# The last two row tiles of a gathered table: written from ScalarE's DMA queue instead of SyncE's, in a four-layer graph network

## The chip, the cores and the metric

The kernel runs on one core of one Trainium2 chip. Its time is the device time of one execution in microseconds. A core has five engines with queues of their own (PE is TensorE, DVE is VectorE, ACT is ScalarE, POOL is GpSimd, SP is SyncE) and 16 DMA engines that all queues share. Here SP and POOL issue DMAs; in the kernel before, ACT issues none.

## The reference

`x` is 2708 x 128, `adj` is 2708 x 2708, both float32. Four layers follow each other, each ending in `x = layernorm(x + layer(x, adj))`. The change lies in the first one:

```python
def _L0_gnn_ref(x, A, W1, b1, W2, b2, sigma, k):      # sigma 1, k 4
    z = _lap_mul(A, x) @ W1 + b1                        # _lap_mul: d * (A @ (d * x)), d = rowsum(A)**-0.5
    z = jax.nn.leaky_relu(z, negative_slope=0.1)
    ...                                                 # d2: squared distances of all rows of z
    S = jnp.exp(-jnp.sqrt(d2 + 1e-10) / (2.0 * sigma))
    S = jnp.where(ranks < k, S, 0.0)                    # the 4 nearest of each row
    A2 = S + A
    out = _lap_mul(A2, x) @ W2 + b2
```

Since `A2 = S + A`, the second product has two parts: the dense `A @ y2`, where `y2` is `x` scaled by the new row sums, and for each row a weighted sum of the rows of `y2` at its four nearest neighbours.

## The kernel before

**Tiling.** The 2708 rows are 22 row tiles (T = 22) of 128 rows, the last one of 20. The columns of the adjacency matrix are cut into six chunks c = 0 to 5 (C = 6) of 512, 512, 512, 512, 384 and 276. Of the transposed matrix the last six row tiles stay in SBUF (`res`); the other 16 (S = 16) are streamed in panels of four row tiles by one chunk, 1024 KB for a chunk of 512, into four slots of a buffer named `ring`. `load_panel` (L171) issues such a load on SP and takes the slots in turn. A slot can be loaded again when PE has read the panel in it.

**Neighbours.** A loop over the row tiles (L628) computes distances on PE, and DVE finds the nearest of each row (L649, L650). `weigh` (L590) turns them into weights and new row sums for a range of row tiles, scales `x` into `y2`, and writes these rows to `y2_rows` in HBM, the table from which neighbours are gathered (the profile calls it `y_rows`, since it leaves buffer numbers out). It is called three times: row tiles 0 to 16, 17 to 19, and last 20 and 21. The first two calls write from POOL's queue. The last call writes from SP's, in two DMAs: row tile 20 (L614, 64 KB) and the 20 rows of tile 21 (L618, 10 KB). Before that, ACT copies the 20 rows to two other partition groups (`spread`, L187).

**The pass over the panels.** `by_panels` (L189) goes through the chunks and, for each, through the row tiles: one product per row tile into the chunk's accumulator (L204), two PE instructions in the profile. For c = 0 four panels were loaded far ahead (`ready`), and the order of the row tiles is 0 to 11, 16 to 19, 12 to 15, 20: the last `y2` rows are needed last. From c = 1 on each panel is loaded into the slot that is freed by the panel four places ahead of it. The first of these loads (c = 1, panel 0, slot 0) is traced inside `with tc.issue_after(behind)`: on SP's queue it stands behind the last write to the table. This sets the order of issue only; it doesn't wait for the write to finish.

**The gather.** `sum_near` (L683) gathers three neighbour rows for each of the 128 rows of a tile with three indirect DMAs from POOL (L677), and DVE adds them up, weighted, into `near_sum` (L690). There are 22 x 3 = 66 gathers, with nine buffers (`got`). The first gather waits until all of the table has landed. When a chunk's products are done, `add_near` (L692) adds `near_sum` of its row tiles to the accumulator on PE (L697); then ACT copies the sum to `hT` (L837) and the linear layer follows (L725). For c = 0 these are row tiles 0 to 3, so gathers 1 to 12. PE, DVE and ACT keep the order that the source writes out here (`manual_schedule`, with the due times of the class `Due`); SP and POOL are ordered by the scheduler.

The order on SP around the change is, in the built program: panel 1 of c = 1 (slot 1), panel 2 (slot 2), the two writes, panel 0 (slot 0), panel 3 (slot 3).

Of the kernel before, what the change touches and what calls it, by code (L numbers as in the profile page):

```python
# [16 lines left out]
P = 128  # L17
# [35 lines left out]
def kernel(  # L53
# [16 lines left out]
    nc = tc.nc  # L70
    N, D = x.shape
    assert D == P
    T = (N + P - 1) // P
# [6 lines left out]
    FULL = N // P  # L80
    LAST = N - FULL * P
    S = T - RES
# [13 lines left out]
    def few(c):  # L96
        g = c % GROUPS * 32
        return slice(g, g + LAST)
# [12 lines left out]
    def acc_tile():  # L111
        return acc_pool.tile([P, CW], F32, tag="acc", name="acc")
# [58 lines left out]
    def load_panel(g, c, pool=None):  # L171

        if pool is None:
            s = slots[taken[0] % len(slots)]
            taken[0] += 1
        else:
            s = pool.tile([P, 4, CW], F32, tag="strip", name="part")
        nc.sync.dma_start(
            s[:, :, : cw[c]],
            adjT[g * 4 * P : (g + 1) * 4 * P, cols[c]].rearrange("(t p) k -> p t k", p=P),  # L180
        )
        return s
# [3 lines left out]
        for g in range(1, GROUPS):  # L186
            (engine or nc.scalar.copy)(rows[few(g)], rows[few(0)])  # L187

    def by_panels(weights, done, tick=None, ready=(), first=None, behind=None):  # L189

        ready = list(ready)
        accs = {}

        def product(c, i, src, w):
            lhsT = weights(i)[few(c) if i == FULL else slice(None)]
            start = c not in accs  # L200
            if start:
                accs[c] = acc_tile()
            stop = tick is None and i == (FULL if c % GROUPS == 0 else FULL - 1)
            nc.tensor.matmul(accs[c][: lhsT.shape[-1], :w], lhsT=lhsT, rhs=src, start=start, stop=stop)  # L204

        for c in range(C):
            w = cw[c]
            for i in [*(first if first and c == 0 else range(FULL)), *([FULL] if c % GROUPS == 0 else [])]:
                if i == FULL:
                    for n in range(c, c + GROUPS):  # L210
                        product(n, i, res[few(n), i - S, cols[n]], cw[n])
                    done(c, accs[c])
                    for _ in range(GROUPS if tick is not None else 0):
                        tick()
                    continue
                if i < S:
                    if i % 4 == 0:
                        if ready:
                            part = ready.pop(0)
                        elif behind is not None:  # L220
                            with tc.issue_after(behind):
                                part = load_panel(i // 4, c)
                            behind = None
                        else:
                            part = load_panel(i // 4, c)
                    src = part[:, i % 4, :w]
                else:
                    src = res[:, i - S, cols[c]]
                product(c, i, src, w)
                if i == FULL - 1 and c % GROUPS:  # L230
                    done(c, accs[c])
                if tick is not None:
                    tick()
# [8 lines left out]
    def rows_of(y):  # L242
        return lambda i: y[:, i, :]
# [122 lines left out]
    y2_rows = dram.tile([N, D], F32, tag="y2_rows", name="y2_rows")  # L366
    xw_rows = dram.tile([N, D], F32, tag="xw_rows", name="xw_rows")
    with tc.tile_pool(name="knn", bufs=1) as knn:
# [68 lines left out]
        due = Due()  # L437
# [28 lines left out]
        with (  # L466
# [5 lines left out]
            for c in range(C):  # L472
# [31 lines left out]
                t0, t1 = ts[0], ts[-1] + 1  # L504
# [53 lines left out]
        y2 = big.tile([P, T, D], F32, tag="y", name="y2")  # L558
# [31 lines left out]
        def weigh(ts):  # L590

            t0, t1 = ts[0], ts[-1] + 1
            nr, sm = near[:, t0:t1, :TOPK], sim[:, t0:t1, :]

            nc.vector.tensor_add(nr, nr, nsq[:, t0:t1, None].to_broadcast([P, t1 - t0, TOPK]))
            nc.vector.tensor_scalar(nr, nr, 0.0, DIST_EPS, op0=ALU.min, op1=ALU.subtract)
            nc.scalar.activation(sm, nr, AF.Ln, scale=-1.0)
            nc.scalar.activation(sm, sm, AF.Exp, scale=0.5)
            nc.scalar.activation(sm, sm, AF.Exp, scale=-0.5)
            dd = d2inv[:, t0:t1]  # L600
            nc.vector.tensor_reduce(dd, sm, AX.X, ALU.add)
            nc.vector.tensor_add(dd, dd, deg[:, t0:t1])  # L602
            nc.scalar.activation(dd, dd, AF.Ln)
            nc.scalar.activation(dd, dd, AF.Exp, scale=-0.5)
            if t1 < T:
                nc.gpsimd.tensor_mul(
                    y2[:, t0:t1, :], xs[:, t0:t1, :], d2inv[:, t0:t1, None].to_broadcast([P, t1 - t0, D])
                )
            else:
                scale_rows(y2, xs, d2inv, ts)  # L610
                spread(y2[:, FULL, :])
            full = min(t1, FULL)
            queue = nc.gpsimd if t1 < T else nc.sync
            ins = queue.dma_start(  # L614
                y2_rows[t0 * P : full * P, :].rearrange("(t p) d -> p t d", p=P), y2[:, t0:full, :]
            )
            if full < t1:
                ins = queue.dma_start(y2_rows[FULL * P :, :], y2[:LAST, FULL, :])  # L618
            else:
                for a in range(t0, t1, 11):  # L620
                    others(range(a, min(a + 11, t1)), nc.gpsimd)
            return ins.ins

        ready = [load_panel(g, 0) for g in range(G)]
        tc.keep_in_program_order(nc.scalar.preload_act_table_set("natural_log_exp_and_others"))
        with tc.tile_pool(name="keys", bufs=3) as keys:

            for n, t in enumerate([*range(4, S), *range(4), *range(S, T)]):  # L628
                p = pw[t]
                z2 = small.tile([P, P], F32, tag="z", name="z2")  # L630
                nc.scalar.mul(z2[:, :p], zT[:, t * P : t * P + p], 2.0)

                key = keys.tile([P, N], F32, tag="key", name="key")
                pks = [acc_tile() for _ in range(C)]
                def norms(c):
                    cs = cols[c]
                    nc.tensor.matmul(pks[c][:p, : cw[c]], lhsT=ones3[:, :p], rhs=nsq3[:, cs], start=True, stop=False)  # L637


                if n:  # L640
                    for c in range(C):
                        norms(c)
                for c in range(C) if n else (5, 3, 2, 4, 1, 0):
                    if not n:
                        norms(c)
                    cs = cols[c]
                    nc.tensor.matmul(pks[c][:p, : cw[c]], lhsT=z2[:, :p], rhs=zT[:, cs], start=False, stop=True)  # L647
                    nc.scalar.copy(key[:p, cs], pks[c][:p, : cw[c]])  # L648
                nc.vector.max(near[:p, t, :], key[:p])  # L649
                nc.vector.max_index(where[:p, t, :], near[:p, t, :], key[:p])  # L650
                if t == T - 6:
                    weigh(range(0, T - 5))
                if t == T - 3:
                    weigh(range(T - 5, T - 2))
            written = weigh(range(T - 2, T))
            others(range(T - 2, T), nc.vector)

    psum.close()
# [162 lines left out]
    due = Due()  # L821
# [50 lines left out]

    with tc.manual_schedule(engines={nc.tensor.engine, nc.vector.engine, nc.scalar.engine}):
        by_panels(
            rows_of(y2), end_pass2, due.tick, ready, [*range(S - 4), *range(S, T - 2), *range(S - 4, S), T - 2], written
        )
        due.flush()
    late.close()
# [6 lines left out]
    ready = [load_panel(g, c) for c, g in panels[: len(slots)]]  # L885
# [15 lines left out]
    with tc.tile_pool(name="rank", bufs=1) as rank:  # L901
# [254 lines left out]
        def weights(lw, n0):  # L1156

            g_all = turned(g_col, n0)
            n1 = min(n0 + 4, NQ)
            m = 2 * (n1 - n0)  # L1160
            b0 = 2 * n0
            w = lw[:, b0 : b0 + m, 2:]
            g = g_all[:, : m * (BJ + 2)].rearrange("p (b j) -> p b j", b=m)[:, :, 2:]
            if n0 // 4 in (1, 3):
                for n in range(m):
                    b = b0 + n
                    nc.scalar.activation(
                        w[:, n], g[:, n], AF.Relu, scale=slot_e[:, b : b + 1], bias=slot_f[:, b : b + 1]
                    )
                return  # L1170
            nc.vector.tensor_mul(w, g, slot_e[:, b0 : b0 + m, None].to_broadcast([P, m, BJ]))
            nc.vector.tensor_add(w, w, slot_f[:, b0 : b0 + m, None].to_broadcast([P, m, BJ]))
            nc.vector.tensor_scalar_max(w, w, 0.0)
# [55 lines left out]
        for c in range(C):  # L1229
            w = cw[c]  # L1230
            begins = c % GROUPS == 0
            for i0 in range(0, FULL - 1, 4):
                if i0 < S:
                    n = c * G + i0 // 4
                    part = ready[n] if n < len(ready) else load_panel(i0 // 4, c)
# [388 lines left out]
```

## Time and profile before

| | us |
|---|---|
| median of three runs | 1066.62 (1063.95 to 1068.74) |
| the profiled execution | 1068.2 |
| its span, first to last instruction | 1066.5 |
| PE busy | 990.4 (93% of the span) |
| DVE, ACT, POOL busy | 643.2, 339.1, 265.6 |
| DMA, mean over the span | 178 GB/s |

The profiled execution is 1.6 above the median and 1.7 longer than its span. All times of instructions below are of this execution, counted from the start of its span. A busy share is a mean over stages with different limits; what the change is worth has to be read from the stage around it, some 50 us from 290 on, in which the pass over the panels begins. In the part of the page that cuts the span in 40 slices, each slice is 26.7 us long; slices 12 and 13 are this stage. Bytes moved there go from 22 GB/s (slice 11) to 199 and 211.

### The profile page before, as it was taken

The page shows a single profiled execution, that of the slowest core. Times are in us where ns is not written, and L with a number is a line of the kernel's source. Part 1 is how long each engine was busy: PE and PEld are TensorE (multiplying, and loading weights), DVE is VectorE, ACT ScalarE, POOL GpSimd, SP SyncE. Part 2 cuts the span into 40 slices and gives each one's busy share as a digit, 9 for nine tenths or more (in the row PEclk, how much of TensorE's full clock was granted, in tenths as well). Part 3 has the DMA queues.
Part 4 walks back from the last instruction along what each step waited for, and adds up shares of the span by engine and source line. Part 5 has one row for each costly group of instructions (what it writes and reads, how often), then busy time and mean ns, then how long its engine had stood idle before and what let it go on. Part 6 is the DMA issues. An engine that isn't in the chain of part 4 may idle for free.

```text
span 1066.5 us, 11423 instructions
## 1 busy us (share of the span) xinstructions
PE 990.4 (93%) x3678; PEld 479.8 (45%) x3678; DVE 643.2 (60%) x1351; ACT 339.1 (32%) x614; POOL 265.6 (25%) x332
## 2 busy tenths in 40 slices
PE   0898999999998999699899999999999999999996
PEld 0345554444434566444333333334444544564444
DVE  5985438999954678764789999995121111132222
ACT  0000125555510235603767777663010100010000
POOL 4000000000447664107774444440121100000000
PEclk9989999999999999699999999999999999999998
DMA  9999350000056756399655546456765856575652
GB/s 338 367 342 249 115 166 1 0 1 1 22 199 211 239 175 207 126 341 306 165 160 131 147 135 164 137 151 208 226 198 173 291 196 202 159 256 170 225 173 67
DMA packets 109363, 190.30 MB, mean 178 GB/s; under 512 B 13650, under 2 KB 46690, under 8 KB 109294
## 3 DMA queue, kind: packets, MB, share of 16 engines
q1 hardware_dynamic: 91582, 151.86, 43.8%
q0 software_dynamic: 17712, 37.62, 12.7%
q8 instruction: 31, 0.51, 0.2%
q14 instruction: 38, 0.31, 0.1%
HBM read 214.37 MB, written 4.16 MB: 205 GB/s over the span
## 4 chain that ended last, share of the span: by engine, by line
PE 80%; DMA 7%; DVE 6%; issue 2%; POOL 2%; ACT 2%; SPq 1%; POOLq 0%; DVEq 0%; ACTq 0%
PE acc L204 34%; PE acc L647 9%; PE hacc L1285 9%; PE num L1428 9%; PE acc L432 7%; DMA res<-in_adjT 3%; PE acc L637 3%; PE acc L1181 2%; DMA got<-y_rows,where 1%; PE mis L289 1%; DMA part<-in_adjT 1%; DVE mask L784 1%; DVE both L487 1%; POOL ring L125 1%; PE mis L1192 1%
## 5 line engine op out<-in xcount | busy, mean ns | idle before, releaser
L1306 POOL DMA_INDIRECT ring<-in_adjT,slot_i x88 | 98.1, 1115 | 101.0 <-PE num L1428 84.8
L1428 PE MATMUL num<-ring,lw 128*64 128x512 f32 (+1 forms) x528 | 113.6, 551 | 3.6 <-DVE err L1270 1.8
L1285 PE MATMUL hacc<-inv,xws 128*128 128x512 f32 (+1 forms) x264 | 111.7, 559 | 0.5 <-ACT inv L1263 0.3
L647 PE MATMUL acc<-zT,z 128*128 128x512 f32 (+4 forms) x264 | 108.5, 558 | 0.0
L1260 ACT ACTIVATE inv<-num,plain 128x1024 f32<-128x1024 f32 x88 | 80.6, 916 | 59.3 <-PE num L1428 58.1
L257 POOL TENSOR_TENSOR rstd<-rstd,minus_half 128x4 f32<-128x4 f32 (+1 forms) x19 | 18.2, 957 | 313.3 <-DVE rstd L256 313.3
L648 ACT COPY key<-acc 128x512 f32<-128x512 f32 (+3 forms) x132 | 70.2, 535 | 59.7 <-issue 29.8
L238 ACT COPY gb<-acc 128x512 f32<-128x512 f32 (+2 forms) x18 | 9.6, 535 | 249.4 <-PE acc L204 249.4
L204 PE MATMUL acc<-ring,y 128*128 128x512 f32 (+2 forms) x192 | 81.8, 555 | 1.6 <-DMA ring<-in_adjT 1.1
L1270 DVE TENSOR_TENSOR err<-inv,num 128x1024 f32<-128x1024 f32 x88 | 74.4, 853 | 13.3 <-ACT inv L1263 12.5
L1285 PEld LDWEIGHTS hacc<-inv,xws 128*128 128x128 f32 x264 | 46.5, 189 | 77.5 <-issue 37.6
L677 POOL DMA_INDIRECT got<-y_rows,where x66 | 70.1, 1063 | 32.8 <-DMA y_rows<-y 9.3
L1277 DVE SCALAR_TENSOR_TENSOR inv<-gb,g_inv,inv 128x1024 f32<-128x1024 f32 x88 | 77.0, 913 | 0.1
L204 PE MATMUL acc<-ring,xs 128*128 128x512 f32 (+2 forms) x192 | 76.7, 542 | 0.0
L204 PE MATMUL acc<-ring,carry 128*128 128x512 f32 (+2 forms) x192 | 74.5, 542 | 0.0
L204 PE MATMUL acc<-ring,m_rows 128*128 128x512 f32 (+2 forms) x192 | 74.3, 542 | 0.0
L1274 DVE SCALAR_TENSOR_TENSOR inv<-err,inv 128x1024 f32<-128x1024 f32 x88 | 72.6, 863 | 0.1
L647 PEld LDWEIGHTS acc<-zT,z 128*128 128x128 f32 (+1 forms) x264 | 47.6, 188 | 54.9 <-issue 49.5
L1263 ACT ACTIVATE inv<-inv 128x1024 f32<-128x1024 f32 x88 | 67.6, 768 | 2.8
L649 DVE MAX8 near<-key 128x8 f32<-128x2708 f32 (+1 forms) x22 | 65.5, 2978 | 4.8 <-ACT key L648 4.8
L574 POOL TENSOR_TENSOR slot_e<-near,sim 128x44 f32<-128x44 f32 (+2 forms) x3 | 0.7, 244 | 271.5 <-DVE d2inv L602 267.3
L650 DVE FIND_INDEX8 where<-near,key 128x8 uint32<-128x2708 f32 (+1 forms) x22 | 65.4, 2972 | 0.0
(327 smaller groups left out, 1340.0 us busy)
## 6 DMA issues: line engine op xcount, KB each, us to landing
ring<-in_adjT SPq DMA_DIRECT2D x86, 1024.0 KB
ring<-in_adjT SPq DMA_DIRECT2D x19, 768.0 KB
part<-in_adjT SPq DMA_DIRECT2D x12, 1024.0 KB
ring<-in_adjT SPq DMA_DIRECT2D x19, 552.0 KB
res<-in_adjT SPq DMA_DIRECT2D x4, 1280.0 KB
more<-in_adjT SPq DMA_DIRECT2D x4, 1024.0 KB
part<-in_adjT SPq DMA_DIRECT2D x3, 768.0 KB
part<-in_adjT SPq DMA_DIRECT2D x3, 552.0 KB
```

What stands on the lines that cost most here:

```text
L204: nc.tensor.matmul(accs[c][: lhsT.shape[-1], :w], lhsT=lhsT, rhs=src, start=start, stop=stop)
L432: nc.tensor.matmul(accs[c][:, : cw[c]], lhsT=y[:, i, :], rhs=src[:, : cw[c]], start=first, stop=last)
L647: nc.tensor.matmul(pks[c][:p, : cw[c]], lhsT=z2[:, :p], rhs=zT[:, cs], start=False, stop=True)
L648: nc.scalar.copy(key[:p, cs], pks[c][:p, : cw[c]])
L677: nc.gpsimd.indirect_dma_start(out=got[:p, :], out_offset=None, in_=y2_rows[:, :], in_offset=bass.IndirectOffsetOnAxis(ap=where[:p, t, k : ...
L1260: nc.scalar.activation(inv, num[:, :w], AF.Ln, scale=plain[:, 0:1], bias=plain[:, 1:2])
L1270: nc.vector.tensor_mul(err, inv, num[:, :w])
L1274: nc.vector.scalar_tensor_tensor(inv, err, 2.0, inv, op0=ALU.subtract, op1=ALU.mult)
L1277: nc.vector.scalar_tensor_tensor(inv, gb[:, col : col + w], g_inv[:, q : q + 1], inv, op0=ALU.max, op1=ALU.mult)
L1285: nc.tensor.matmul(haccs[:, o:e], lhsT=xws[:, q, :], rhs=inv[:, o:e], start=(q == 0), stop=(q == NQ - 1))
L1306: nc.gpsimd.indirect_dma_start(out=rows[i][:KC, n, :], out_offset=None, in_=adj_half[:, :], in_offset=bass.IndirectOffsetOnAxis(ap=slot_i[ ...
L1428: nc.tensor.matmul(num[n * (BJ + 2) : (n + 1) * (BJ + 2), o:e], lhsT=lw[:, 2 * q + n, :], rhs=rows[i][:, n, c0 + o : c0 + e], start=True, ...
```

## The change

The last call of `weigh` writes from ACT's queue instead of SP's. `weigh` no longer hands back its last DMA, `by_panels` loses the parameter `behind`, and the first load of c = 1 is an ordinary `load_panel`.

```diff
-    def by_panels(weights, done, tick=None, ready=(), first=None, behind=None):
+    def by_panels(weights, done, tick=None, ready=(), first=None):
...
                         if ready:
                             part = ready.pop(0)
-                        elif behind is not None:
-                            with tc.issue_after(behind):
-                                part = load_panel(i // 4, c)
-                            behind = None
                         else:
                             part = load_panel(i // 4, c)
...
-            queue = nc.gpsimd if t1 < T else nc.sync
-            ins = queue.dma_start(
+            queue = nc.gpsimd if t1 < T else nc.scalar
+            queue.dma_start(
                 y2_rows[t0 * P : full * P, :].rearrange("(t p) d -> p t d", p=P), y2[:, t0:full, :]
             )
             if full < t1:
-                ins = queue.dma_start(y2_rows[FULL * P :, :], y2[:LAST, FULL, :])
+                queue.dma_start(y2_rows[FULL * P :, :], y2[:LAST, FULL, :])
...
-            return ins.ins
...
-            written = weigh(range(T - 2, T))
+            weigh(range(T - 2, T))
...
-            rows_of(y2), end_pass2, due.tick, ready, [*range(S - 4), *range(S, T - 2), *range(S - 4, S), T - 2], written
+            rows_of(y2), end_pass2, due.tick, ready, [*range(S - 4), *range(S, T - 2), *range(S - 4, S), T - 2]
```

In the built program SP now issues the panels of c = 1 in the order 0, 1, 2, 3. ACT issues the two writes right behind the two copies of `spread` and ahead of the copy L837. The order of all other instructions on PE, DVE, ACT and POOL is the same.

## The prediction

> **What bounds the kernel now.** The page's first part says PE:
>
> ```profile
> span 1066.5 us, 11423 instructions
> PE 990.4 (93%) x3678; PEld 479.8 (45%) x3678; DVE 643.2 (60%) x1351; ACT 339.1 (32%) x614; POOL 265.6 (25%) x332
> ```
>
> So the change can pay only where PE stands still. The waits of 280 to 345 us, the stage around the change, show where (waiting engine and line, what it waited for; us, times, longest):
>
> ```profile
> ACT hT L837 <- PE acc L697: 29.3, 1, 29.3
> ...
> POOL got L677 <- DMA y_rows<-y: 9.3, 1, 9.3
> ...
> PE acc L697 <- DVE near_sum L690: 4.0, 1, 4.0
> ...
> PE acc L204 <- DMA ring<-in_adjT: 1.1, 1, 1.1
> ```
>
> PE waits twice: 1.1 us for a panel and 4.0 us for the gathered sums of c = 0. Third view: the chain of waits in this stretch, which names the origin of the longer one (start, us, what):
>
> ```profile
> 294.84 10.55 PE acc L204 x24
> ...
> 305.41 0.37 SPq L178
> ...
> 305.83 0.50 SPq L614
> ...
> 306.38 6.41 DMA y_rows<-y
> ...
> 313.68 0.31 POOL got L677
> ...
> 319.04 5.45 DMA got<-y_rows,where
> ...
> 326.85 6.18 DMA got<-y_rows,where
> ...
> 333.92 0.49 PE acc L697 x2
> ```
>
> Read it downwards. The write of tile 20 stands on SP behind the load of slot 2, which waits until PE has read that slot (305.4). Both writes land at 306.38 + 6.41 = 312.8. POOL then starts the gathers (313.68), one each 1.30 us; the eleventh takes 6.2 us to land, and PE goes on at 333.92. So **the write, and not PE, sets the time here**. The panel wait is in PE's timeline:
>
> ```profile
> 312.08 2.09 PE L204 MATMUL acc<-res,y 128*128 128x512 f32 x8
> 315.30 14.00 PE L204 MATMUL acc<-ring,y 128*128 128x512 f32 x32 [1.13 <-DMA ring<-in_adjT]
> 329.14 0.83 PE L697 MATMUL acc<-ident,near_sum 128*128 128x128 f32 x6
> 333.92 0.49 PE L697 MATMUL acc<-ident,near_sum 128*128 128x128 f32 x2 [3.95 <-DVE near_sum L690]
> ```
>
> Last, stretches of 1 us behind the second wait (span, length, busy of the engines, then PE's granted clock, DMA share, GB/s):
>
> ```profile
> 335.00:336.00 1.00, 1.00 (x3) 0.49 (x2) 0.10 (x1) 0.98 (x2) 0.70 (x2) 0.68 0.36 123
> 336.00:337.00 1.00, 1.00 (x4) 0.48 (x4) 0.64 (x2) 0.34 (x1) 0.96 (x1) 0.50 0.29 82
> 337.00:338.00 1.00, 1.00 (x6) 1.00 (x6) 0.40 (x1) 0.00 (x0) 0.74 (x1) 0.50 0.23 57
> 338.00:339.00 1.00, 1.00 (x5) 0.64 (x4) 0.49 (x2) 0.00 (x0) 0.69 (x2) 0.61 0.08 25
> ```
>
> The wait has an after-effect: 0.32 + 0.50 + 0.50 + 0.39 = **1.7 us** of PE time lost to a halved clock. In this trace gaps of 1.13, 1.82 (at 515) and 1.87 us (735) leave the clock at 1.00; gaps of 2.16 (417), 2.30 (461) and 3.95 halve it. From about 2 us of idling on, it costs 1.7 more.
>
> [...] No run of before shows ACT's ring. [...] the panel in front of the write had moved its bytes by about 310 (383 + 240 + 389 + 379 GB/s in the four microseconds from 306), the write landed 2.7 us later.
>
> **The change, part by part.**
>
> *Panel 0 of c = 1 goes first.* PE frees slot 0 after four of the first twelve row tiles: 294.84 + 4 x 10.55/12 = 298.4. SP is idle then and issues at once, instead of at 306.78. The DMA moves 0 GB/s from 300 to 303, so nothing is in its way. A panel of 1.05 MB at the 400 GB/s of 310 to 312 takes 2.6 us[...]: it lands near 305 and is needed at 314.17. **PE's wait of 1.13 us goes**, and PE reaches L697's last two matmuls (row tile 3) at 329.97 - 1.13 = 328.84. Panels 1 and 2 keep their times (slots 1 and 2 free at 302.0 and 305.4), panel 3 (312.1) too. By itself this brings nothing: PE would wait 5.1 us for the sums instead of 3.95.
>
> *The two writes on ACT.* ACT ends the copies L187 at 305.1 and issues there (0.50 and 0.36 us, SP's durations): start 305.15 and 305.7 instead of 305.83 and 306.38. The waits that the built program gives them are on loads for c = 0, long landed: the page shows 0 to 1 GB/s from 160 to 267. Behind them on ACT stands only the copy L837, which PE releases at 334.4; with 29.3 us of idling there, 0.9 us of issue costs nothing. SP loses the same 0.9, free too.
>
> *When do the writes land?* Not shown in the trace, so bounded. Lower: like a gather of 64 KB with nothing beside it (2.6 us from issue, the fourth: 317.73 to 320.3), 305.7 + 2.9 = 308.6. POOL's own write of 192 KB (issued 303.47; the similar L768 write of 256 KB takes 4.1) is in by about 308, so it doesn't gate. Upper: the slot 2 panel (issued 305.41) goes first on each engine, and the write lands 2.5 us after its last byte at 310.1: 312.6, as before. Between: gathers that become ready while a panel flows take 5.0 to 6.2 us, giving 310.7 to 311.9. I take **310.5**, a little below these since the first write is issued before slot 2's load. The first gather then starts 0.87 later, as now: 311.4 instead of 313.7, **2.3 us earlier**.
>
> *What the gathers make of it.* The twelfth is issued at 328.16 - 2.3 = 325.9. In the way are the panels of c = 2, issued when PE frees slots, now from 317.6, 321.1, 324.5 and 328.0, that is 1.13 earlier than before. Relative to them the gathers gain 1.2 us. If all gathers keep their delays, the sums are ready 2.3 us earlier, 331.6; if they slip before the fourth panel, up to 1 more. I take 2.6: PE goes on at **331.3**. Its gap is then 331.3 - 328.84 = 2.5 us, above 2, so the half clock stays. Up to here no gain is counted twice: the 1.13 lies inside the 2.6.
>
> *Behind it.* From 334 to 415 PE is busy throughout (20.0 of 20 us in each stretch from 340 to 400), and DVE, ACT, the slots of the ring and the later gathers (from the 37th on they wait for free buffers) hang on PE or on the same first gather, so they move along. No late thing in the way: the sums of c = 1 are used at 355.1, their last gather was issued at 343.8. I keep 2.6, and 0.3 more for the chance that the gap falls below 2 us: **3 us**.
>
> Sum: 1066.5 - 3 = 1063.5 for the span, 1065.2 for the profiled execution of 1068.2. That one stood 1.6 above the median, so for a median I subtract the 3 from 1066.6: **1063.6**. The runs of before spread by 4.8 us; what a measurement can tell from no change is about 0.5%, 5.3 us.
>
> **The rivals.**
>
> *Early write.* Both writes pass between the panels of slots 1 and 2 and land at 309.5 or before. Gathers start 3.3 us earlier or more, the twelfth is out before 325 and the sums are there by 330.7. PE's gap falls below 2 us, the clock stays full: 3.2 + 1.7 = 4.9, at most 5.1 + 1.7 = 6.8. Time 1060 to 1061.7. For it: slot 2's load follows the first write only by a little on the engines. Against it: the second write is issued after that load.
>
> *Hidden anyway.* The write gets its turn only behind slot 2's panel and lands near 312.6. Then the gathers gain 0.2, at most 1.1 with the panels: 1065.5 to 1066.4. [...] This is also how the change would fail to do what it says.
>
> *Starved write, slower.* On ACT's own ring the write is no longer ahead of any panel. If the engines pass it over until the panel of slot 3 (issued 312.1, bytes 314.0 to 316.8) is through, it lands at 316.8 + 2.5 = 319.3 and everything behind it is 6.5 late; in exchange the gathers then meet fewer panels and the last ones take 2.7 instead of 5.3 to 6.2, so PE goes on near 337.5: 3.6 slower, 1070. One more panel, 3.4 us apart, and it is 7 slower, 1073.6. The point is a landing at 312.8. Against it: the DMA is idle of panels from about 310 to 314 now.
>
> **How the numbers follow.** Forecast as above (gain 1.5 to 4.5): 0.45. Early write: 0.25. Hidden: 0.15. Starved: 0.15. Faster by over 5.3 us: half of the early cases and their spread in measurement, with the upper edge of the forecast, 0.27. Slower by over 5.3: the starved cases of two panels, and one panel with an unlucky spread, 0.15. Within: 0.58. The range takes the early case to its end and the starved one to its first step: 1059 to 1070.5.
>
> **What would show it.** Right: no wait L204 <- DMA ring near 314; the chain still goes through the write, now from ACT, landing at 309 to 312; first gather near 311.4; PE on L697 after a gap of 2 to 3 us; half clock behind it. Wrong: a landing after 312.8; a gap of 4 us or more on L697; or the gain up to 340 lost again by 440.

## The result, and the profile after

Nine runs of the changed kernel have a median of 1061.78 us (1059.55 to 1066.67); nine of the kernel before, on the same chip, have 1068.75 (1063.95 to 1073.10). The ratio is 0.9937, with a 95% interval of 0.9918 to 0.9957: **6.7 us faster, at least 4.6 and at most 8.8**. The forecast was 3.

The first part of the page, and one row of its DMA queues (packets, MB, share):

```profile
span 1064.9 us, 11424 instructions
PE 993.3 (93%) x3678; PEld 481.3 (45%) x3678; DVE 642.9 (60%) x1351; ACT 338.8 (32%) x614; POOL 266.7 (25%) x332
...
q10 hardware_dynamic: 174, 0.08, 0.0%
```

The queue q10 is new: the 74 KB of the two writes, on ACT's own queue. The span is only 1.6 shorter, since the profiled execution (1066.67) is the slowest of its nine; the end of this section shows where it loses time. First the waits of the stage, 280 to 345 us (us, times, longest):

```profile
ACT hT L832 <- PE acc L692: 23.9, 1, 23.9
DVE near_sum L685 <- DMA got<-y_rows,where: 17.1, 10, 4.2
...
POOL got L672 <- DMA y_rows<-y: 4.5, 1, 4.5
```

POOL waits 4.5 us for the table instead of 9.3. No row of PE waiting for the sums or for a panel is left. The chain of waits from 294 to 340 says the same: of write and gathers nothing stands in it.

```profile
293.35 33.26 PE acc L204 x80
326.60 0.89 PE acc L692 x8
327.50 1.72 PE acc L204 x4
329.21 0.89 PE mis L720 x8
```

Next ACT's, POOL's, DVE's and PE's timelines, from which the times of the steps are read (start, us, engine, line; in brackets the idle time before it):

```profile
302.98 0.30 ACT L187 COPY y<-y 20x128 f32<-20x128 f32 x1 [0.49 <-DVE y L260]
302.99 0.34 ACTq L610 DMA_DIRECT2D y_rows<-y  x1
303.30 0.30 ACT L187 COPY y<-y 20x128 f32<-20x128 f32 x1
303.38 0.61 ACTq L614 DMA_DIRECT2D y_rows<-y  x1
327.53 0.58 ACT L832 COPY hT<-acc 128x512 f32<-128x512 f32 x1 [23.94 <-PE acc L692]
...
307.39 1.14 POOL L672 DMA_INDIRECT got<-y_rows,where  x1 [4.55 <-DMA y_rows<-y]
...
326.20 0.74 DVE L685 SCALAR_TENSOR_TENSOR near_sum<-got,sim,near_sum 128x128 f32<-128x128 f32 x2 [0.20 <-DMA got<-y_rows,where]
...
312.60 14.00 PE L204 MATMUL acc<-ring,y 128*128 128x512 f32 x32
326.44 1.05 PE L692 MATMUL acc<-ident,near_sum 128*128 128x128 f32 x8
327.33 1.88 PE L204 MATMUL acc<-res,y 128*128 128x512 f32 x4
```

The pass over the panels begins at 293.35 here and at 294.84 before; another kernel that is the same up to there begins at 293.19, so the change isn't the cause. From here on a time with a plus is counted **from the start of the pass**, PE's first product on L204, so that executions can be compared. ACT issues at +9.64 and +10.03, with the first copy and not behind the copies. The first gather starts at +14.04 instead of +18.84. The last two sums of row tile 3 end at 326.20 + 0.74 = 326.94, or +33.59, where PE went on at +39.08 before. PE reaches these two matmuls near 327.1, after six of the eight, with no gap: **the sums come 0.2 us before they are needed**. PE's transposes L737 start at +42.60, those of before (L742) at +49.69, **7.1 us earlier**. That is 1.13 of panel wait, 3.95 of waiting for sums, 1.7 of half clock, and 0.3 of small pieces, for this pair of executions; how far others differ is told with the experiments.

One-microsecond stretches of the same execution (PE's granted clock is the third value from the end):

```profile
327.00:328.00 1.00, 1.00 (x7) 0.72 (x6) 0.14 (x1) 0.47 (x1) 0.82 (x1) 1.00 1.11 406
328.00:329.00 1.00, 1.00 (x3) 0.38 (x2) 0.02 (x1) 0.98 (x2) 0.70 (x2) 1.00 0.98 260
...
460.00:461.00 1.00, 1.00 (x9) 1.00 (x8) 1.00 (x2) 0.00 (x0) 0.00 (x0) 0.75 1.05 389
461.00:462.00 1.00, 1.00 (x7) 1.00 (x6) 1.00 (x2) 0.00 (x0) 0.00 (x0) 0.50 1.04 387
...
967.00:968.00 1.00, 1.00 (x3) 0.40 (x3) 0.00 (x0) 0.00 (x0) 0.00 (x0) 0.50 0.00 0
```

Behind the sums the clock stays at 1.00. But this execution has half clock from 460 to 468 and again from 965 to 973, with PE busy all the time. The trace of before has neither; what it has at 461 comes directly behind a gap of 2.30 us, and its counterpart here, behind a gap of 2.16, is from 453 to 457. Added up over all stretches of a microsecond from 290 on (one minus the clock, times PE's busy time), the half clock costs 16.0 us here and 10.5 before; these two take 3.4 each. Without them, by this estimate, the execution would have taken 1066.67 - 6.8 = 1059.9, close to the fastest of the nine. So the lead of the stage isn't given to another wait: in this one execution it is taken back by a clock that falls elsewhere, with no gap of PE directly ahead of it. At 417 of before, the first gap of PE behind the pass, the lead is whole: the same matmul stands at +122.44 before and at +115.36 after, still 7.1.

### The profile page after: what moved, and what is told of

The parts are those of the page before. It is cut to its first block, busy times and chain, and to the rows that moved or that the text cites. A ratio compares the mean times of both kernels' runs of the same rounds, so it can differ in the third digit from the quotient of the medians.

```text
span 1064.9 us, 11424 instructions
## 1 busy us (share of the span) xinstructions
PE 993.3 (93%) x3678; PEld 481.3 (45%) x3678; DVE 642.9 (60%) x1351; ACT 338.8 (32%) x614; POOL 266.7 (25%) x332
## 4 chain that ended last, share of the span: by engine, by line
PE 81%; DVE 5%; DMA 5%; POOL 3%; issue 3%; ACT 2%; SPq 1%; POOLq 0%; DVEq 0%; ACTq 0%
PE acc L204 36%; PE acc L642 9%; PE hacc L1280 9%; PE num L1423 8%; PE acc L428 7%; DMA res<-in_adjT 3%; PE acc L1176 2%; PE acc L632 2%; PE mis L285 1%; DMA part<-in_adjT 1%; DVE mask L779 1%; DMA ring<-in_adjT,slot_i 1%; DVE both L483 1%; POOL ring L125 1%; PE mis L1187 1%
## 5 line engine op out<-in xcount | busy, mean ns | idle before, releaser
L204 PE MATMUL acc<-ring,y 128*128 128x512 f32 (+2 forms) x192 | 82.0, 557 | 0.5 <-POOL sim L579 0.5
L204 PE MATMUL acc<-ring,xs 128*128 128x512 f32 (+2 forms) x192 | 78.2, 551 | 0.0
L204 PE MATMUL acc<-ring,carry 128*128 128x512 f32 (+2 forms) x192 | 74.5, 542 | 0.0
L204 PE MATMUL acc<-ring,m_rows 128*128 128x512 f32 (+2 forms) x192 | 74.3, 542 | 0.0
```

## The experiments

The theory after the result: what counts is that the write is on its way **before the load of slot 2**, which is issued when PE has freed that slot (+10.57 in before). ACT's queue brings it there. Rivals: ACT's own queue as such; the early load of panel 0, which no longer stands behind the writes on SP. All kernels were timed beside the kernel before (median 1068.81 of 37 runs for the first four, 1068.61 of 59 for the others).

| | first write, second write | first gather | PE's gap on the sums | transposes | ratio, 95% | us |
|---|---|---|---|---|---|---|
| before | SP +10.99, +11.54 | +18.84 | 3.95 | +49.69 | | |
| after | ACT +9.64, +10.03 | +14.04 | none | +42.60 | 0.9937 (0.9918 to 0.9957) | -6.7 |
| e1_sp_no_order | SP +10.99, +11.54 | +18.03 | 2.85 | +47.72 | 0.9993 (0.9979 to 1.0006) | -0.7 |
| e2_act_panel0_late | ACT +9.64, +10.03 | +14.15 | none | +44.14 | 0.9943 (0.9922 to 0.9964) | -6.1 |
| e3_sp_write_first | SP +9.63, +10.03 | +12.45 | none | +42.60 | 0.9956 (0.9930 to 0.9983) | -4.7 |
| e4_pool | POOL +9.91, +10.49 | +16.46 | 2.65 | +47.22 | 0.9965 (0.9951 to 0.9980) | -3.7 |
| e5_act_late | ACT +9.64 (10 KB), +12.55 (64 KB) | +17.50 | 3.83 | +48.38 | 0.9999 (0.9985 to 1.0012) | -0.1 |
| e6_filled_gap | SP +10.99, +11.53 | +17.95 | 0.66 behind the filling | +47.26 | 0.9991 (0.9975 to 1.0007) | -1.0 |
| e7_add_later | SP +10.99, +11.53 | +16.86 | none | +47.76 | 0.9950 (0.9924 to 0.9977) | -5.3 |
| e8_after_add_later | ACT +9.64, +10.03 | +14.07 | none | +47.76 | 0.9964 (0.9949 to 0.9979) | -3.8 |

The last column is (ratio - 1) times the median of before. For e1 to e6 it and the column of the transposes agree within the interval; that of e3 is the loosest (7.1 in the trace, 1.8 to 7.5 in time). In e7 and e8 the transposes have six more row tiles ahead of them, so their column can't be compared.

One trace of before is a thin base. In e6 and e7, SP issues the panels and the writes around this place at the same times as in before (within 0.01 us), and yet the table lands earlier (POOL's timelines of e6 and e7):

```profile
312.58 1.14 POOL L677 DMA_INDIRECT got<-y_rows,where  x1 [8.45 <-DMA y_rows<-y]
...
311.71 1.14 POOL L677 DMA_INDIRECT got<-y_rows,where  x1 [7.35 <-DMA y_rows<-y]
```

The first gather starts at +17.95 and +16.86 there, against +18.84 in before, and PE's panel wait is 0.23 us in e6 and missing in e7. With the write from ACT (after, e2, e8) it is +14.04 to +14.15. So before is the slowest of three executions in this stage: the change brings the first gather forward by 2.7 to 4.8 us, and 7.1 us is what this pair of traces gives, not a constant.

**e1_sp_no_order**: panel 0 freed from the writes, but the writes on SP as before (diff against the changed kernel).

```diff
-            queue = nc.gpsimd if t1 < T else nc.scalar
+            queue = nc.gpsimd if t1 < T else nc.sync
```

> The writes stay on SP, but the load of panel 0 of c = 1 no longer stands behind them (SP's order: panels 0, 1, 2, the two writes, panel 3). Theory 'place of the write': PE's wait of 1.1 us for the panel goes, the write still stands behind panel 2's load and lands about 8 to 9 us after DVE has the rows of y2 (before 8.8, after 4.0), PE's gap at L692 grows to about 5 us, the half clock stays: 0 to 1 us faster than before. Rival 'order of the panels': the freed panel load is what pays, so at least 1.1 us and up to half of the 6.7 us measured, 2 to 4 us faster.

SP's timeline and PE's wait of this kernel:

```profile
300.33 3.80 SPq L178 DMA_DIRECT2D ring<-in_adjT  x2
304.18 0.50 SPq L610 DMA_DIRECT2D y_rows<-y  x1
304.73 0.36 SPq L614 DMA_DIRECT2D y_rows<-y  x1
...
330.27 0.49 PE L692 MATMUL acc<-ident,near_sum 128*128 128x128 f32 x2 [2.85 <-DVE near_sum L685]
```

The panel wait is gone, and PE still waits for the sums, which come 2 us earlier (+37.08 against +39.08). The gap did not grow to 5 us, as expected, but shrank to 2.85. How much of this is the freed panel and how much the spread between executions, one trace can't say: the first gather, at +18.03, lies within the +16.86 to +18.84 of before, e6 and e7. In the time nothing shows. This half of the change, alone, brings at most 2.2 us.

**e2_act_panel0_late**: the writes on ACT as in the change, but panel 0 of c = 1 is issued behind panels 1 and 2 (diff against the changed kernel, cut; `loads` collects the DMAs of `load_panel`).

```diff
+                        elif first and c == 1 and i == 0:
+                            n = taken[0]
+                            taken[0] = n + 1
+                            ready = [load_panel(g, c) for g in (1, 2)]
+                            taken[0] = n
+                            with tc.issue_after(loads[-1]):
+                                part = load_panel(0, c)
+                            taken[0] = n + 3
```

> The writes go from ACT as in the changed kernel, but panel 0 of c = 1 is queued on SP behind panels 1 and 2, as before the change. Theory 'place of the write': the write lands about 4 us after DVE has the rows, no gap above 1 us at L692 and no half clock there; a wait of 0 to 1 us for the panel comes back near 314: 5.5 to 7 us faster than before. Rival 'order of the panels': without it the gain is at most half, 3 us or less.

```profile
314.31 14.00 PE L206 MATMUL acc<-ring,y 128*128 128x512 f32 x32 [1.28 <-DMA ring<-in_adjT]
328.14 1.24 PE L702 MATMUL acc<-ident,near_sum 128*128 128x128 f32 x8
```

PE's timeline again: the panel wait is back, with 1.28 us, and behind it no gap for the sums. So the other half, the early write, carries nearly all of the gain: 6.1 us in time, 5.6 in the trace.

**e3_sp_write_first**: the kernel before, with the writes on SP, but with the first three panels of c = 1 behind them.

```diff
-                        elif behind is not None:
+                        elif behind is not None and c == 1 and i < 12:
                             with tc.issue_after(behind):
                                 part = load_panel(i // 4, c)
-                            behind = None
```

> The writes stay on SP but stand ahead of the loads of panels 0, 1 and 2 of c = 1 (in the kernel before only panel 0 is behind them). Theory 'place of the write': nothing is ahead of the writes, they land about 4 us after DVE has the rows; panel 0 is issued at about 306 and lands by 312, before its need at 314; 6 to 7 us faster than before, like the changed kernel. Rival 'ring of its own': only another ring than the panels' gets the write through; in SP's ring, with 3 MB of panels right behind it, it lands later than 6 us after the rows, and the gain is 3 us or less.

SP's and POOL's timelines:

```profile
303.83 0.35 SPq L613 DMA_DIRECT2D y_rows<-y  x1
304.23 0.38 SPq L617 DMA_DIRECT2D y_rows<-y  x1
304.71 1.49 SPq L178 DMA_DIRECT2D ring<-in_adjT  x3
...
306.65 1.44 POOL L676 DMA_INDIRECT got<-y_rows,where  x1 [2.95 <-DMA y_rows<-y]
```

SP's queue does it too: same times of issue as on ACT, gathers even 1.6 us earlier. The difference between the two is that here the loads of panels 0 and 1 stand behind the write as well: the first of them is issued at 304.71, and from 304 to 306 the DMA moves 303 KB, little more than the three writes to the table (272 KB), so hardly any of a panel passes with the write. PE's transposes start at +42.60, as in the change: with no gap left, earlier sums are worth nothing. So **ACT's queue isn't needed: a write issued as early, ahead of the panels, does it on SP**.

**e4_pool**: the last call of `weigh` writes from POOL's queue, like the first two (`queue = nc.gpsimd`).

> The last two row tiles are written from POOL's queue, like the rest of the table, with SP's panel order of the changed kernel. Theory 'place of the write': POOL is idle there, the writes have no panel ahead of them; two issues of about 0.9 us each instead of ACT's 0.3 and 0.6, so they land about 5 us after the rows of y2 are there, 1 us later than from ACT; gap at L692 about 1 us, no half clock: 5 to 6.5 us faster than before. Rival 'ring of its own': POOL's ring also carries its 192 KB write of row tiles 17 to 19, issued 1 us earlier, so the writes land at 7 us or more; half the gain, 3 us.

```profile
303.22 0.58 POOL L610 DMA_DIRECT2D y_rows<-y  x1 [0.40 <-DVE slot_e L578]
303.80 0.57 POOL L614 DMA_DIRECT2D y_rows<-y  x1
309.77 1.13 POOL L672 DMA_INDIRECT got<-y_rows,where  x1 [5.40 <-DMA y_rows<-y]
...
329.90 0.78 PE L692 MATMUL acc<-ident,near_sum 128*128 128x128 f32 x2 [2.65 <-DVE near_sum L685]
330.47 3.32 PE L204 MATMUL acc<-res,y 128*128 128x512 f32 x4
```

POOL's and PE's timelines. It issues only 0.3 and 0.5 us later than ACT, but the rows land 2.4 us later (first gather +16.46), and PE gets a gap of 2.65 with a half clock behind it: four matmuls of L204 take 3.32 us instead of 1.88. Whether the delay comes from POOL's own 192 KB write before them or from slot 2's load, issued in the same microsecond, no run tells apart. The expectation (a gap of about 1 us, no half clock) missed, and issuing ahead of slot 2's load is not always enough: both writes are issued before it (+10.57), and still land late. This is the outcome that the prediction gave to the change, gap, half clock and gain (3.7 us).

**e5_act_late**: the change, but seven idle copies on ACT (L609, in place) hold the 64 KB write back until 2.0 us after the issue of slot 2's load (+10.57).

```diff
                 spread(y2[:, FULL, :])
+                for _ in range(7):
+                    nc.scalar.copy(y2[:, t0, :], y2[:, t0, :])
```

> The changed kernel, with seven copies of row tile 20 of y2 onto itself on ACT ahead of its write (L610's), each waiting for the one before: the 64 KB write is issued some 2 to 3 us later, at about 12 us after the start of the pass, behind the issue of panel 2's load (10.6) instead of ahead of it (9.6). [...] it lands 3 to 4.5 us after issue, first gather at 16 to 17.5 us after the start of the pass (before 18.8, after 14.0), gap at L692 about 2 to 3 us with the half clock: 2 to 4 us faster than before. Rival 'a panel that flows is drained first, ACT's ring or not': it lands behind panel 2 as SP's write does, first gather at 18 us or more, gap about 4 us: 0 to 2 us faster than before.

```profile
302.42 2.28 ACT L609 COPY y<-y 128x128 f32<-128x128 f32 x7
304.72 0.36 ACTq L612 DMA_DIRECT2D y_rows<-y  x1
...
309.67 1.14 POOL L674 DMA_INDIRECT got<-y_rows,where  x1 [8.00 <-DMA y_rows<-y]
...
329.93 0.49 PE L694 MATMUL acc<-ident,near_sum 128*128 128x128 f32 x2 [3.83 <-DVE near_sum L687]
```

ACT's, POOL's and PE's timelines. Issued 2.5 us later than the second write of the change, on the same queue, the rows land 3.5 later (first gather +17.50 against +14.04), PE waits 3.83 us, and the gain is gone: 0.9999. Gap and gain are those of the rival, not the 2 to 3 us of gap and 2 to 4 us of gain that the expectation names first. Together with e3: **ACT with a late write brings nothing, SP with an early one brings the gain**. Whether the later issue or the place behind a panel does the harm, e5 doesn't separate: 2.5 of its 3.5 us are later issue (1.0 later even than before), and 1.0 is a longer transfer. From the second issue to the landing it is 3.1 to 3.3 us ahead of slot 2's load on ACT (after, e2, e8), 4.1 behind it on ACT (e5), and 4.5 to 6.4 behind it on SP (e7, e6, e1, before). A write from ACT right behind slot 2's load was not run.

**e6_filled_gap**: the kernel before, with four matmuls into a spare bank (3.6 us, result not used) ahead of row tile 3's sums, so that PE doesn't stand still. It isolates the half clock behind the gap.

```diff
+            if c == 0 and t == ts[-1]:
+                fill = mis_tile()
+                for _ in range(4):
+                    nc.tensor.matmul(fill, lhsT=ident, rhs=res[:, 0, :CW], start=True, stop=True)
```

> The kernel before, with four idle matmuls of 512 columns (8 PE instructions, 3.4 us) put on PE between the add of row tile 2 and that of row tile 3 of c = 0, where PE waits for the sums. Their result is not used. The wait shrinks to about 0.5 us, nothing is issued earlier. Theory 'the half clock is a part of the gain': clock 1.00 behind the wait, 1.7 us faster than before (1.0 to 2.0), with the sums as late as before. Rival 'the half clock has nothing to do with the gap': the stretch of 3.4 us at half clock stays, no change.

```profile
328.69 3.60 PE L700 MATMUL mis<-res,ident 128*128 128x512 f32 x8
332.95 0.49 PE L701 MATMUL acc<-ident,near_sum 128*128 128x128 f32 x2 [0.66 <-DVE near_sum L690]
333.27 1.88 PE L204 MATMUL acc<-res,y 128*128 128x512 f32 x4
```

PE's timeline: with 0.66 us of gap left, the four matmuls behind it take 1.88 (2.51 in before). From the sums to the transposes it is 47.26 - 38.32 = 8.94 us, against 49.69 - 39.08 = 10.61 in before. The half clock thus costs **1.67 us**, as the prediction read it from the clock (1.7). In the total (-1.0, from -2.7 to +0.7) it can't be told from nothing.

**e7_add_later** and **e8_after_add_later**: the kernel before, and the changed one, with `add_near` of c = 0 placed six row tiles later in PE's order, so that the sums have 5.2 us more.

```diff
-        n = max(due.n + 1, near_at[chunk_tiles[c][-1]] + 3, ended[-1] + 16)
+        n = max(due.n + 1, near_at[chunk_tiles[c][-1]] + 3, ended[-1] + 16) + (6 if c == 0 else 0)
```

> The kernel before, with the sums of c = 0 added on PE six row tiles of c = 2 later (6 x 0.86 = 5.2 us of other products first); the writes stay where they are. Theory 'late sums stop PE': the gap of 3.95 us and the half clock behind it (1.7) go, the wait of 1.1 us for the panel stays: 5 to 6 us faster than before without moving the write. Rival 'what comes after the sums is as late as before' (linear, norm, ranks of c = 0, and the later chunks are due a fixed number of tiles after it): the work of DVE behind it ends the pass as late as before, 0 to 2 us.

> The changed kernel, with the sums of c = 0 added six row tiles later as well. Theory 'late sums stop PE': in the changed kernel no gap is left in its trace, so nothing more is gained there: 6 to 7.5 us faster than before, as the changed kernel is. Rival 'the changed kernel still waits in many executions, since its sums come only just in time': up to 1.5 us faster than the changed kernel, 7.5 to 8.5 faster than before. Rival 'the work behind is shifted': slower than the changed kernel by up to 5 us.

PE's timeline of the second:

```profile
332.97 1.05 PE L692 MATMUL acc<-ident,near_sum 128*128 128x128 f32 x8
...
360.74 0.23 PE L797 MATMUL rk<-ones_b,mask 128*128 128x1 bf16 x3 [1.86 <-DVE mask L779]
```

In both, the transposes start at +47.76, which is 42.60 plus the six row tiles of 0.86 us that PE has done before. So without touching the write, the later place removes the wait and its after-effect too (e7: 5.3 us faster). The panel wait, expected to stay, isn't in e7's trace. But DVE then gets `hT`'s successors later, and PE waits 1.66 (e7) and 1.86 us (e8) for DVE's mask at 361, a wait that the changed kernel doesn't have. On top of the change it is no gain: 3.8 us against 6.7, with intervals that just overlap. It looks like the last case of its expectation (the work behind is shifted). None of these kernels is measured faster than the changed one; e2's 6.1 can't be told from its 6.7.

## Why the prediction was right and wrong

**Right: the chain.** That the write and not PE set the time, by way of the table, the gathers and the sums, is what e2 and e3 (early write, from ACT and from SP) and e5 (late write) show from both sides. The panel wait went (that panel 0 lands near 305 was the author's estimate; in after its load is issued at 297.05, and the DMA moves 1097 KB from 298 to 302, for a panel of 1049), and its going alone brought nothing that can be told from noise (e1). ACT's two issues were free (23.9 us of idling before its copy L832). The gain went on whole to 417, as the step "Behind it" had it. The half clock's price was right (e6); its rule, that gaps from about 2 us on halve the clock, was not (last section).

**Wrong: the landing of the write.** The term "310.5" in the sum was too late. The landing, taken as 0.87 before the first gather, was 306.5 in the trace of after, 308.0 on the clock of before. That is 2.5 us earlier than taken and 0.6 earlier than the lower bound of 308.6 (which adds 2.9 where the gather that it is read from took 2.6). Two parts of the term failed:

- *Issue.* The step let ACT issue after its copies L187, at 305.15 and 305.7. In fact the first write is issued together with the first copy: it wasn't held back until the copies ahead of it had ended. On the clock of before the issues are 304.5 and 304.9. That is 0.7 and 0.8 us, but it turns the order: slot 2's load is issued at 305.41, so both writes are ahead of it, where the prediction had the second behind.
- *Transfer.* From the second issue to the landing the prediction allowed 4.8 us, its author's estimate for a write with that panel beside it. It took 306.52 - 303.38 = 3.1. Behind the panel (e5) it is 4.1 from issue, still less than allowed; with hardly any of a panel beside it (e3) it is 306.65 - 0.87 - 304.23 = 1.6, so the 2.5 to 2.7 us that the prediction set between the last byte of a panel and a landing are no fixed price.

From there the working held. The prediction gave the sums 0.3 more than the landing; they gained 5.4 (333.87 in before, +39.03, against +33.59) with a landing 4.8 earlier. Its rival "Early write" priced this case at 4.9 to 6.8 us, from the same terms (3.2 to 5.1 of waits, 1.7 of clock): 7.1 in the trace, 6.7 in time. It had a quarter of the chance, for the reason "the second write is issued after that load", which was the wrong step.

**The rest.** "Hidden anyway" had the write land near 312.6, as from SP. It didn't: the saving begins with the time of issue, 1.5 us (+11.54 to +10.03), but the write then also takes less from issue to landing (3.1 against 6.4 us), and lands 4.8 us earlier in this pair of traces. "Starved write" didn't come: on its own queue the write was not passed over until the next panel, even behind slot 2's (e5: 4.1 us from issue to landing). Whether it helps there to have a queue of its own, no run shows: on SP's queue the write behind the panel took hardly longer in e7 (4.5).

The predicted 1063.6 lies near the measured 1061.78 partly by luck: the forecast gain was 3.7 us too small, and the median of before was 1068.75 over nine runs, 2.1 more than over the three it started from, which hides 2.1 of it.

## What to carry to other kernels

Where a small write gates a long chain, ask what is issued within the microseconds around it, on any queue: here 1.5 us of issue, which took it ahead of a 1 MB load, was worth 2.7 to 4.8 us of landing, and a different queue with a later issue, behind that load, was worth nothing. Two waits in a row on one engine must be priced together: removing the first alone can hand its time to the second (e1: no gain in time). Before splitting a gain into parts, look at a second execution of the same instructions: here the landing alone moved by 2.0 us. And when a gap closes by a hair (0.2 us here), what is left to gain at that place is nothing, so look at the next one.

## What the runs showed of the hardware

**A DMA on ACT's queue can overtake the computing before it.** The first write's issue starts at 302.99, 0.01 us after the start of the first copy, which takes 0.30, and before the second copy (303.30), though both copies stand ahead of it in the built program. A write of what the computing makes is still held back: in e5 the 64 KB write is issued at 304.72, when the seven copies end (302.42 + 2.28 = 304.70).

**Around 2 us, a gap halves the clock only in some executions.** The prediction read from one trace that gaps of 2.16 us halve the clock and gaps of 1.87 don't. PE's wait for DVE's mask behind the pass (L802 in before) lasts 2.15 to 2.17 us in eight of the ten traces. Half clock (0.50 granted) follows it in four of them (before, after, e2, e6) and not in the other four (e1, e3, e4, e5: 1.00 up to 422); in e7 and e8 it lasts 1.97, and the clock is halved in e8 alone, only from 414 on (0.50 at 415 and 416), 1.6 us after the wait has ended. Two stretches of e3 behind its wait (which ends at 409.54), in which the clock stays at 1.00:

```profile
410.00:411.00 1.00, 1.00 (x8) 0.78 (x6) 0.93 (x3) 1.00 (x4) 0.00 (x0) 1.00 1.06 410
411.00:412.00 1.00, 1.00 (x8) 0.85 (x6) 0.87 (x4) 1.00 (x1) 0.74 (x1) 1.00 0.64 244
```

Gaps of 2.65 us and more on the sums (e4, e1, e5, before) halved it each time: the four matmuls of L204 behind them took 3.32, 3.42, 3.25 and 2.51 us, against 1.88 at full clock. At 2.15 to 2.17 us, then, the outcome varies; what decides it these ten traces don't show.

**The clock also falls without a gap, in steps of 1.7 us.** The loss at 460 to 469 is nothing in e6 and e8, 1.7 in e1, e2, e3 and e5, and 3.4 in after, e4 and e7; that near 968 is nothing in before, e1, e3, e5 and e8, 1.7 in e2, e6 and e7, and 3.4 in after and e4. In after PE has no gap directly ahead of either. The two executions with 3.4 at both places are slow for their kernels (e4's took 1069.07, its median is 1065.82); e3's, with 8.8 us lost in all, took 1059.78. What sets the clock off there stays open. Two profiled executions can differ by 7 us in this way, so a change of this size has to be read in its stage and in the median.
